# First head pair from all tokens, kept tokens chosen by 0/1 products, in masked attention on one core

## Chip, cores and metric

The kernel runs on one core of one Trainium2 chip. The core has TensorE (PE), with its weight loads shown on a row of their own (PEld), VectorE (DVE), ScalarE (ACT), GpSimd (POOL) and SyncE (SP), which here only issues DMAs. The metric is the device time of one execution in microseconds (us); the runs of the kernel before took 684.1, 685.0 and 688.35 us, median 685.0.

## The reference, cut to what matters

```python
B, D, T = x.shape                      # 8, 512, 1024, float32; NH = 8 heads of dk = 64
xt = jnp.transpose(x, (0, 2, 1))
q = xt @ Wq.T                          # one projection serves as queries, keys and values
qh = q.reshape(B, T, NH, dk).transpose(0, 2, 1, 3)
scores = scale * jnp.einsum('bhqd,bhkd->bhqk', qh, qh)
logits = (scores * cmask + (1.0 - cmask) * NEG) * rmask     # mask is 0 or 1
attn = jax.nn.softmax(logits, axis=-1)
ctx = jnp.einsum('bhqk,bhkd->bhqd', attn, qh)
out = ctx.transpose(0, 2, 1, 3).reshape(B, T, D) @ Wo.T
return x + jnp.transpose(out, (0, 2, 1))
```

About half of the 1024 tokens of a batch are kept (mask 1). All tokens that are not kept attend evenly to all tokens, so one column, the mean of x, stands for all of them.

## The kernel before

**Path.** `early` (L1014) counts the kept tokens of every batch. `late(n)` (L1137) computes with n columns a batch: up to n-1 kept tokens and the mean's column. n is 544 (`SHORT`) here, or 576 (`LONG`) in another branch; if neither fits, or if a sum of exponentials underflows, the general kernel is run at the end. Every engine reads `verdict` and branches between `early` and `late`. With n = 544 the columns lie in two halves of 272, and in four key chunks of 128 and one short chunk (`LAST`).

**Batches and pairs.** Heads are taken two at a time (128 rows). `pairs` holds 8 batches x 4 pairs; `p` counts them, `pr` is the pair in its batch `b`. A pair takes five steps k, one for each key chunk, the short one first. In a step `scores` puts q.q products into PSUM (tag `s`, two tiles of two banks; all other products share four banks of tag `t`), ACT takes exp of them, and then `slots_of(p)` and the tables after L1160 say what else is issued in the step: projecting and transposing a coming pair (`project`, `values`, `lengths_of`, `bias_of`), weighing the values of the pair before, output products, and the loading, transposing, gathering and fetching of other batches. This order is written out by hand; each engine runs its instructions in it. The second pair starts with the second row of L648, the short chunk's scores.

**The tokens of a batch.** Tokens are transposed to rows in DRAM (`xd`), the index of each kept token is found (`search`, DVE, by ranks), POOL gathers the rows by an indirect DMA (`gather`), PE transposes them back into `xc` (`collect`), and `project` multiplies by wqT. For batches 1 to 7 this runs beside the pairs of the batch before.

**The first batch.** Nothing runs beside it. `early` loads x of batch 0 on SP (L379, eight pieces of 256 KB), makes ranks (L1087), transposes all tokens (`turn_first`, L401: 32 transposes on PE, copies on ACT, stores on SP), sums features (`mean_first`, DVE) and searches. `late` loads wq on POOL, brings its columns into order (`order_columns`, ACT, L999), gathers, collects, transposes wq (`turn_weights`, L1009), projects pair 0 and half of pair 1, and only then begins the steps of pair 0.

**Number format.** All is float32. A plain product is recorded as two passes on PE, each with a weight load of its own; a transpose is recorded as one.

Of the kernel before, what the change touches and what calls it, by code (L numbers as in the profile page):

```python
# [19 lines left out]
NEG = -1e30  # L20
# [286 lines left out]
def attention_of_kept_tokens(ctx, tc, x, mask, wq, wo, out, ident, wqT, woT, verdict, flag):  # L307
# [52 lines left out]
    homes = [keep.tile([B * NT, P], F32, name=f"home_{i}") for i in range(2)]  # L360
    seen = {}
# [39 lines left out]
    def turn_first(i):  # L401

        r, at = divmod(i * P, NB)
        pt = bank(f"xt_0_{i}")
        for d in range(ND):
            nc.tensor.transpose(pt[:, d * P : (d + 1) * P], xs[0][r][:, d, at : at + P], ident)  # L406
# [58 lines left out]
    def place_ranks(b):  # L465
        rank = sb.tile([P, T], F32, tag="rank", name=f"rank_{b}", bufs=1)
        found = sb.tile([P, NC], F32, tag="found", name=f"found_{b}")
        if b:
            source = sb.tile([P, NC], I32, tag="source", name=f"source_{b}")
        else:  # L470
            source = keep.tile([P, NC], I32, name="source_0")
# [36 lines left out]
    def collect(b, i):  # L508
# [11 lines left out]
        )  # L520

# [79 lines left out]
    def bias_of(pair):  # L601
# [7 lines left out]
        biases[pair] = sb.tile([P, NC], F32, tag="bias", name=f"bias_{b}_{pr}")  # L609
# [325 lines left out]
    def slots_of(p):  # L935

        b, pr = pairs[p]
# [8 lines left out]
        if p == 0:  # L946
            todo[0].append(lambda: project(behind, 1))
            todo[1].append(lambda: values(behind))
        if behind:
            if p == 0:  # L950
                todo[2].append(lambda: lengths_of(behind))
            elif p != ND - 1:
                todo[1].insert(0, lambda: lengths_of(behind))
# [448 lines left out]
```

## Time and profile before

| | us |
|---|---|
| median of 3 runs | 685.0 |
| profiled execution | 689.0 |
| its span on the core | 687.3 |
| PE idle in the span | 41.7 |
| first scores of pair 0 (L648) | 40.06 |
| first scores of pair 1 | 58.11 |
| first scores of pair 2 | 72.97 |
| POOL's first gather | 22.90 |
| ACT's first instruction in `late` | 21.98 |

A page of the profile shows one execution. Busy times are unions over an engine's instructions. In the list by time, a row gives start, duration, engine, source line, operation, output and inputs, shapes and count, and in brackets the idle time before it with what ended it; rows of like instructions are merged, so the duration of a row with xN is that of all N. A matmul's recorded duration includes its way through the array, so the pace of a series is read from start to start. The clock column is TensorE's granted clock, 1.00 at full speed.

### The profile page before, as it was taken

Reading aid. Unit: us, or ns where it says so; the run is one execution under the profiler, and the core shown is the slowest. Engines: PE = TensorE matmul, PEld = TensorE weight load, DVE = VectorE, ACT = ScalarE, POOL = GpSimd, SP = SyncE. Lnnn points to the kernel's source line nnn. Section 1 sums busy time; section 2 is a strip of 40 time slices with the busy share of each in tenths; the row PEclk is TensorE's granted clock in tenths of the full one; section 3 lists DMA queues with packets and bytes.
Section 4 is the critical chain, followed back from the end, with each engine's and each line's share of the span. In section 5 each row is a group of like instructions: output and inputs, shape, how many; then the busy total and the mean of one; then the engine's idle time right before and its main releaser. Section 6 shows DMA issues by size and latency. Waiting matters only on the chain.

```text
span 687.3 us, 12044 instructions
## 1 busy us (share of the span) xinstructions
PE 645.6 (94%) x4139; PEld 391.5 (57%) x4139; DVE 359.4 (52%) x1049; ACT 397.2 (58%) x1059; POOL 182.5 (27%) x306
## 2 busy tenths in 40 slices
PE   6489999999999999999999999999999999999953
PEld 5456566656565655556565655555565656554422
DVE  5235676335464654747464654836564434724462
ACT  4566668755584657655584656665675556454400
POOL 3540310130044202450144202450144102334040
PEclk9799999999999999999999999999999999999985
DMA  6473832451766568854876477865764473339358
GB/s 230 155 240 90 253 89 68 141 158 45 169 182 212 155 171 209 269 181 115 210 191 207 156 182 193 261 193 137 190 195 127 114 184 100 113 119 251 84 174 260
DMA packets 96969, 116.37 MB, mean 169 GB/s; under 512 B 10312, under 2 KB 74312, under 8 KB 96896
## 3 DMA queue, kind: packets, MB, share of 16 engines
q1 hardware_dynamic: 80144, 75.13, 40.4%
q0 software_dynamic: 12528, 38.25, 17.4%
q10 hardware_dynamic: 4224, 2.10, 1.0%
q8 instruction: 35, 0.57, 0.3%
q14 instruction: 38, 0.31, 0.1%
HBM read 72.78 MB, written 42.67 MB: 168 GB/s over the span
## 4 chain that ended last, share of the span: by engine, by line
PE 84%; DMA 6%; ACT 3%; DVE 2%; issue 2%; SPq 1%; POOL 1%; POOLq 0%; ACTq 0%; DVEq 0%
PE s L626 21%; PE av L672 19%; PE pq L544 16%; PE po L793 14%; PE s L648 3%; PE xc L513 3%; PE v L569 2%; PE pa L821 2%; PE top L605 1%; ACT e L634 1%; DMA xr<-in_x_dram 1%; DMA xd<-xt 1%; DMA row<-rt 1%; DMA g<-od,origin 1%; PE xt L406 1%
## 5 line engine op out<-in xcount | busy, mean ns | idle before, releaser
L634 ACT ACTIVATE e<-s,bias 128x544 f32<-128x544 f32 x256 | 180.4, 710 | 69.4 <-PE s L626 63.2
L626 PE MATMUL s<-qT 64*128 64x272 f32 x1024 | 170.1, 417 | 2.9 <-ACT el L651 1.0
L626 PEld LDWEIGHTS s<-qT 64*128 64x128 f32 x1024 | 97.7, 186 | 70.6 <-issue 28.9
L672 PE MATMUL av<-e,v 128*64 128x272 f32 x1024 | 131.4, 399 | 0.0
L544 PE MATMUL pq<-xc,wqT 128*128 128x272 f32 x512 | 124.8, 397 | 0.0
L544 PEld LDWEIGHTS pq<-xc,wqT 128*128 128x128 f32 x512 | 97.4, 195 | 18.6 <-issue 0.8
L793 PE MATMUL po<-woT,cT 128*128 128x512 f32 (+1 forms) x448 | 107.5, 434 | 0.0
L672 PEld LDWEIGHTS av<-e,v 128*64 128x64 f32 x1024 | 67.9, 136 | 56.0 <-issue 23.1
L805 POOL DMA_DIRECT2D od<-oc x56 | 30.2, 551 | 251.3 <-ACT oc L803 251.1
L793 PEld LDWEIGHTS po<-woT,cT 128*128 128x128 f32 (+1 forms) x448 | 46.9, 150 | 46.9 <-issue 46.1
L907 POOL DMA_INDIRECT g<-od,block_origin x56 | 57.0, 1017 | 27.1 <-issue 12.4
L867 DVE STREAM_TRANSPOSE o<-g 128x512 f32<-128x512 f32 x56 | 39.3, 702 | 42.6 <-DMA g<-od,block_origin 42.6
L651 ACT ACTIVATE el<-s,bias 128x544 f32<-128x544 f32 x32 | 22.8, 714 | 59.8 <-PE s L648 44.9
L663 DVE CUSTOM_DVE_ANT_0 junk<-el,part 128x272 f32<-128x272 f32 x64 | 28.3, 442 | 53.4 <-ACT el L651 41.2
L592 DVE TENSOR_REDUCE len<-sq 128x10 f32<-128x640 f32 x32 | 26.2, 818 | 52.3 <-ACT sq L590 52.3
L552 ACT COPY qT<-pq 128x272 f32<-128x272 f32 x64 | 24.4, 381 | 49.9 <-PE pq L544 48.3
L903 POOL COPY step<-e 1x1 f32<-1x1 f32 x77 | 15.9, 206 | 136.2 <-ACT e L634 105.7
L634 ACT ACTIVATION_READ_ACCUMULATOR e<-s,bias 128x1 f32 x256 | 50.3, 197 | 0.0
L500 POOL DMA_INDIRECT xin<-xd,source x40 | 39.5, 987 | 20.3 <-issue 6.9
L870 DVE TENSOR_TENSOR xr<-o,xr 128x512 f32<-128x512 f32 x56 | 38.8, 693 | 9.9 <-DMA xr<-in_x_dram 6.9
L607 DVE TENSOR_REDUCE m<-top 128x1 f32<-128x128 f32 x32 | 9.3, 291 | 63.4 <-PE top L605 63.4
L488 DVE TENSOR_SCALAR_CACHE_REDUCE junk<-rank,key 128x1024 f32<-128x1024 f32 (+4 forms) x40 | 40.0, 999 | 3.4 <-ACT rank L1094 2.4
(147 smaller groups left out, 671.0 us busy)
## 6 DMA issues: line engine op xcount, KB each, us to landing
x<-in_x_dram SPq DMA_DIRECT2D x56, 256.0 KB
xd<-xt SPq DMA_DIRECT2D x112, 128.0 KB
xr<-in_x_dram SPq DMA_DIRECT2D x28, 512.0 KB
out_dram<-xr SPq DMA_DIRECT2D x24, 512.0 KB
rb<-row SPq DMA_DIRECT2D x60, 160.0 KB
od<-oc POOLq DMA_DIRECT2D x28, 256.0 KB
rank<-ranks SPq DMA_DIRECT2D x6, 512.0 KB
xd<-xt SPq DMA_DIRECT2D x8, 256.0 KB
```

What stands on the lines that cost most here:

```text
L488: nc.vector.tensor_scalar(junk[:, :n], rank[:, i * P :], key[:, col], 0.0, ALU.is_le, ALU.add, accum_out=found[:, col])
L500: nc.gpsimd.indirect_dma_start(out=xin[:n, :], out_offset=None, in_=xds[b], in_offset=bass.IndirectOffsetOnAxis(ap=searches[b][2][:n, i : ...
L544: nc.tensor.matmul(pq[:, :KH], wqT[:, d, pr * P : (pr + 1) * P], xcs[b][:, d, cols], start=(d == 0), stop=(d == ND - 1),)
L626: nc.tensor.matmul(ss[h][:, hf, :KH], qT[heads[h], keys], qT[heads[h], queries[hf]], start=True, stop=True,)
L634: nc.scalar.activation(e[:, :, h, :], ss[h][:, :, :KH], AF.Exp, bias=bias, scale=SCALE, accum_out=sums[pair[1] % 2][:, h, c : c + 1],)
L663: nc.vector.tensor_tensor_reduce(junk[:, :KH], e[:, 0, h, :], parts[b], 1.0, 0.0, ALU.mult, ALU.add, ends[pr % 2][:, h : h + 1])
L672: nc.tensor.matmul(av[head, :KH], v[keys, c, head], e[keys, hf if c < LAST else 0, h, :], start=(c == first), stop=(c == last),)
L793: nc.tensor.matmul(po[k * n : (k + 1) * n, :w], cTs[b, pr][:, i * P : i * P + n], woT[:, pr, k * w : (k + 1) * w], start=(pr == 0), stop=( ...
L805: nc.gpsimd.dma_start(ods[b][places[i], k * w : (k + 1) * w], oc[k * n : (k + 1) * n, :w])
L867: nc.vector.transpose(o.rearrange("p k t -> p (k t)"), gs[b, i])
L870: nc.vector.tensor_tensor(to, o, to, ALU.add)
L907: nc.gpsimd.indirect_dma_start(out=g, out_offset=None, in_=ods[b], in_offset=bass.IndirectOffsetOnAxis(ap=block_origin[:, b, i : i + 1], a ...
```

## The change

- x of batch 0 is loaded second half first, behind the first 128 rows of wq; the other rows of wq follow. They go into the room of `woT`.
- Pair 0 is projected from all 1024 tokens (`project_all`, eight blocks of 128 tokens) with those 128 rows of wq, transposed. DVE builds 0/1 matrices that say which token goes to which column (`choose`), and PE multiplies the projected blocks by them (`choose_of`) into `rings[0]`. The squares of all projected tokens give the pair's bias.
- The indices of the kept tokens come from products of the 0/1 matrices with a column of token numbers, and the mean of x from products of the transposed tokens with a column of ones (`tokens_of_first`). The ranks' broadcast, the search and the feature sums of batch 0 go.
- `late` begins with the steps of pair 0. Transposing wq, collecting the gathered tokens, projecting pairs 1 and 2 and the mean's column for pair 0 are issued within them. The projection of pair (1, 0) moves from the third pair to the fourth, and batch 1's loads, features, turns, gathers and collects move later by some steps.
- wq's columns are ordered on POOL; batch 1 is loaded on SP.
- The branch is taken on `fit < 544` alone; the 576 path is run behind it, inside the branch that holds the general kernel.

```diff
+    def load_first():
+
+        xs[0] = [sb.tile([P, ND, NB], F32, tag="x", name=f"x_0_{r}", bufs=NN) for r in range(NN)]
+        for r in reversed(range(NN)):
+            for d in range(ND):
+                nc.sync.dma_start(
+                    xs[0][r][:, d, :],
+                    x[0].rearrange("(p d) t -> d p t", d=ND)[d][..., r * NB : (r + 1) * NB],
+                )
+
+    def first_block(i):
         r, at = divmod(i * P, NB)
+        return [xs[0][r][:, d, at : at + P] for d in range(ND)]
...
-        for d in range(ND):
-            nc.tensor.transpose(pt[:, d * P : (d + 1) * P], xs[0][r][:, d, at : at + P], ident)
-        if i == 0:
-            xds[0] = dr.tile([T + 1, D], F32, tag="xd_0", name="xd_0", bufs=1)
-            nc.sync.dma_start(xds[0][T : T + 1, :], zero)
+        for d, block in enumerate(first_block(i)):
+            nc.tensor.transpose(pt[:, d * P : (d + 1) * P], block, ident)
         tag = "oc" if i < NC else "xin"
-        xt = sb.tile([P, D], F32, tag=tag, name=f"xt_0_{i}", bufs=NC)
-        nc.scalar.copy(
+        xt = firsts[i] = sb.tile([P, D], F32, tag=tag, name=f"xt_0_{i}", bufs=NC)
+        engine(
             xt.rearrange("p (a d f) -> p a d f", a=A, d=ND),
             pt.rearrange("p (d a f) -> p a d f", d=ND, a=A),
         )
         nc.sync.dma_start(xds[0][i * P : (i + 1) * P, :], xt)
 
-    def mean_first():
-        xbars[0] = keep.tile([P, ND, NN], F32, name="xbar_0")
-        for r in range(NN):
-            nc.vector.tensor_reduce(xbars[0][:, :, r], xs[0][r], axis=AX.X, op=ALU.add)
...
+    def choose(i, S):
+
+        nc.vector.tensor_scalar(S, count[:, : S.shape[1]], place[:, i : i + 1], None, ALU.is_equal)
...
+    def tokens_of_first(chosen, ones):
+
+        pt = bank("source_0")
+        for i in range(NC):
+            n = min(P, LONG - i * P)
+            for c in reversed(range(i, NT)):
+                nc.tensor.matmul(
+                    pt[:n, i : i + 1],
+                    chosen[c][:, i * P : i * P + n],
+                    since[:, c : c + 1],
+                    start=(c == NT - 1),
+                    stop=(c == i),
+                )
+        source = keep.tile([P, NC], I32, name="source_0")
+        nc.vector.tensor_scalar(source[:, :LAST], pt[:, :LAST], float(T), None, ALU.add)
+        nc.vector.tensor_scalar(source[:DK, LAST:NC], pt[:DK, LAST:NC], float(T), None, ALU.add)
+        searches[0] = None, None, source
+        pm = bank("mean_0")
+        for a in range(A):
+            for i in range(NT):
+                nc.tensor.matmul(
+                    pm[:, a : a + 1],
+                    firsts[i][:, a * P : (a + 1) * P],
+                    ones[:, 0:1],
+                    start=(i == 0),
+                    stop=(i == NT - 1),
+                )
+        nc.scalar.mul(first_mean, pm[:, :A], 1.0 / T)
...
+    def project_first(chosen, mcol):
+
+        wT = sb.tile([P, ND, P], F32, tag="junka", name="wqT_0", bufs=1)
+        pw = bank("wq_0_t")
+        for d in range(ND):
+            nc.tensor.transpose(pw[:, d * P : (d + 1) * P], woT[:, 0, d::ND], ident)
+        nc.scalar.copy(wT.rearrange("p d e -> p (d e)"), pw)
...
+        def project_all(i):
+            r, at = divmod(i * P, NB)
+            for d, block in enumerate(first_block(i)):
+                nc.tensor.matmul(
+                    tall[:, r, at : at + P], block, wT[:, d, :], start=(d == 0), stop=(d == ND - 1)
+                )
+
+        def copy_two(i):
+            r, at = divmod(i * P, NB)
+            nc.scalar.copy(
+                q[:, i : i + 2, :].rearrange("p c e -> p (c e)"), tall[:, r, at : at + 2 * P]
+            )
...
+        def choose_of(i):
+            w = chosen[i].shape[1]
+            for hf in range(2):
+                n = min(w - hf * H, H)
+                if n > 0:
+                    nc.tensor.matmul(
+                        short[:, hf, :n],
+                        q[:, i, :],
+                        chosen[i][:, hf * H : hf * H + n],
+                        start=(i == NT - 1),
+                        stop=(i * P <= hf * H),
+                    )
+
+        copy = nc.scalar.copy
+        for i in (7, 6, 5, 4):
+            project_all(i)
+            if i % 2 == 0:
+                copy_two(i)
+        turn_first(7, copy)
+        choose_of(7)
+        choose_of(6)
+        turn_first(6, copy)
+        square(1)
+        choose_of(5)
+        choose_of(4)
+        lengths(1)
+        turn_first(5, copy)
+        turn_first(4, copy)
+        for i in (3, 2, 1, 0):
+            project_all(i)
+            if i % 2 == 0:
+                copy_two(i)
+        for i in (3, 2, 1, 0):
+            choose_of(i)
+        square(0)
+        lengths(0)
+        nc.scalar.copy(
+            rings[0][:, :LONG].rearrange("p (h n) -> p h n", h=2), short[:, :, :H]
+        )
+        nc.vector.tensor_tensor(
+            first_len,
+            first_len,
+            mcol[:, :NT].unsqueeze(2).to_broadcast([P, NT, 2]),
+            ALU.mult,
+        )
+        nc.vector.tensor_reduce(
+            first_top, first_len.rearrange("p c h -> p (c h)"), axis=AX.X, op=ALU.max
+        )
+        turn_first(3, nc.vector.tensor_copy)
+        tops[pairs[0]] = first_top
+        bias_of(pairs[0], first_bias)
+        for i in (2, 1, 0):
+            turn_first(i, nc.vector.tensor_copy)
...
+    def put_first_mean():
+
+        xcs[0] = sb.tile([P, ND, NK], F32, tag="xc", name="xc_0", bufs=1)
+        nc.scalar.copy(xcs[0][:, :, NK - 1], first_mean)
+
+    def project_first_mean():
+
+        pq = bank("mean_0_0")
+        for d in range(ND):
+            nc.tensor.matmul(
+                pq[:, 0:1],
+                wqT[:, d, 0:P],
+                xcs[0][:, d, NK - 1 : NK],
+                start=(d == 0),
+                stop=(d == ND - 1),
+            )
+        nc.scalar.copy(rings[0][:, W - 1 : W], pq[:, 0:1])
...
         late = p == 2
         if pr == 2 and b + 1 < B:
-            at = (2, 2, 2, 3, 3) if late else (1, 2, 2, 2, 2)
+            at = (3, 3, 4, 4, 4) if late else (1, 2, 2, 2, 2)
             todo[at[0]].append(lambda: put_mean(b + 1))
             for i in range(NC):
                 todo[at[i]].append(lambda i=i: collect(b + 1, i))
+        if p == 0:
+            for d in range(ND):
+                todo[d // 2].append(lambda d=d: turn_weights(wqT, "wq", d))
+            todo[2].append(lambda: values(pair))
+            todo[2].append(put_first_mean)
+            for i in range(NC):
+                todo[(3, 3, 4, 4, 4)[i]].append(lambda i=i: collect(0, i))
+            for hf in range(2):
+                todo[4].append(lambda hf=hf: project(behind, hf))
+            todo[4].append(lambda: values(behind))
+            todo[4].append(lambda: lengths_of(behind))
+            for hf in range(2):
+                todo[4].append(lambda hf=hf: project(ahead, hf))
+            todo[4].append(project_first_mean)
+            todo[4].append(lambda: bias_of(behind))
+        elif p == 1:
+            todo[0].insert(0, lambda: values(behind))
+        elif p == ND - 1:
+            for hf in range(2):
+                todo[1 + hf].append(lambda hf=hf: project(behind, hf))
...
-        if ahead:
+        if ahead and p and not late:
             for hf in range(2):
-                todo[4 if late else 3].append(lambda hf=hf: project(ahead, hf))
-        if ahead and not late:
+                todo[3].append(lambda hf=hf: project(ahead, hf))
...
-            nc.scalar.copy(
+            nc.gpsimd.tensor_copy(
...
-        load_batch(0)
+        nc.sync.dma_start(woT[:, 0, :], wq[0:P, :])
+        load_first()
+        for e in range(1, ND):
+            nc.sync.dma_start(woT[:, e, :], wq[e * P : (e + 1) * P, :])
...
+        pc = bank("place_t")
+        nc.tensor.matmul(pc[:, :NT], upto, mcol[:, :NT], start=True, stop=False)
+        nc.tensor.matmul(
+            pc[:, :NT], spread[:, 0, :], before[:, 0, :], start=False, stop=True
+        )
...
+        room = room.rearrange("p k n -> p (k n)")
+        chosen, end = {}, 0
+        for i in reversed(range(NT)):
+            n = min((i + 1) * P, LONG)
+            chosen[i] = room[:, end : end + n]
+            end += n
+            choose(i, chosen[i])
...
+        project_first(chosen, mcol)
+        tokens_of_first(chosen, ones)
...
-        weights["wq"] = order_columns(load_weights(wq, "wq", nc.gpsimd), "wq")
+        queries_of(0)
+        load_batch(1)
+        weights["wq"] = order_columns([woT[:, e, :] for e in range(ND)], "wq")
+        for qT in rings[1:]:
+            nc.gpsimd.memset(qT[:, NK - 1 : NK], 0.0)
         for i in range(NC):
             gather(0, i)
-        queries_of(0)
-        for qT in rings:
-            nc.gpsimd.memset(qT[:, NK - 1 : NK], 0.0)
-        load_batch(1, nc.gpsimd)
         load_ranks(1, nc.gpsimd)
-        put_mean(0)
-        for i in range(NC):
-            collect(0, i)
-            if i < ND:
-                turn_weights(wqT, "wq", i)
         weights["wo"] = load_weights(wo, "wo", nc.gpsimd)
-        for hf in range(2):
-            project(pairs[0], hf)
-        values(pairs[0])
-        lengths_of(pairs[0])
-        project(pairs[1], 0)
+        qT = qTs[pairs[0]] = rings[0]
+        biases[pairs[0]] = first_bias
+        nc.vector.tensor_copy(
+            qT[:, NK:W].rearrange("p (r k) -> p r k", k=END),
+            qT[:, NK - END : NK].unsqueeze(1).to_broadcast([P, (W - NK) // END, END]),
+        )
...
+        LOAD_LATER = {(2, 1): (0, 1), (2, 2): (2, 3), (2, 3): (4, 5), (2, 4): (6, 7)}
+        TURN_LATER = [(0, 4), (1, 0), (1, 1), (1, 2)]
...
+        FEATURES_LATER = {(1, 1): (0,), (1, 2): (1,), (1, 3): (2,), (1, 4): (3,), (2, 0): (4, 5), (2, 1): (6, 7)}
...
+        GATHER_LATER = {(1, 4): (0,), (2, 0): (1,), (2, 1): (2,), (2, 2): (3,), (2, 3): (4,)}
...
-    with ExitStack() as pools:
-        early, late = attention_of_kept_tokens(
-            pools, tc, x, mask, wq, wo, out, ident, wqT, woT, verdict, flag
-        )
-        with tc.manual_schedule():
-            early()
-        fit = nc.values_load(verdict[0:1, 0:1], min_val=0, max_val=2 * T)
-        with tc.If(fit > SHORT - 1, label="over") as over:
-            with tc.If(fit < LONG):
+    def kept_tokens(n):
+
+        with ExitStack() as pools:
+            early, late = attention_of_kept_tokens(
+                pools, tc, x, mask, wq, wo, out, ident, wqT, woT, verdict, flag
+            )
+            with tc.manual_schedule():
+                early()
+            fit = nc.values_load(verdict[0:1, 0:1], min_val=0, max_val=2 * T)
+            with tc.If(fit < n):
                 with tc.manual_schedule():
-                    late(LONG)
-        with over.Else():
-            with tc.manual_schedule():
-                late(SHORT)
+                    late(n)
+
+    kept_tokens(SHORT)
     again = nc.values_load(flag[0:1, 0:1], min_val=0, max_val=1)
     with tc.If(again > 0, label="again"):
-        turn_all_weights(tc, [(wq, wqT), (wo, woT)], ident)
-        attention_of_all_tokens(tc, x, mask, out, ident, wqT, woT)
+        kept_tokens(LONG)
+        again = nc.values_load(flag[0:1, 0:1], min_val=0, max_val=1)
+        with tc.If(again > 0):
+            turn_all_weights(tc, [(wq, wqT), (wo, woT)], ident)
+            attention_of_all_tokens(tc, x, mask, out, ident, wqT, woT)
```

More of the change, by code (lines that the diff above doesn't have):

```diff
@@ L935, in slots_of @@
     def slots_of(p):
-        b, pr = pairs[p]
+        b, pr = pair = pairs[p]
         todo = [[] for _ in range(NC)]
@@ L1079, in early @@
         seen["mrow"], seen["rank"] = mrow, rank
-        tc.mark_branch_hint_location("over", "LikelyTaken", engines=ENGINES)
-        place_ranks(0)
-        for r in range(NN):
-            pt = bank(f"rank_{r}")
-            for i in range(G):
-                chunk = r * G + i
-                nc.tensor.matmul(
-                    pt[:, i * P : (i + 1) * P],
-                    ident[:BC, chunk : chunk + 1].to_broadcast([BC, P]),
-                    rank,
-                    start=True,
-                    stop=True,
-                )
-            nc.scalar.copy(searches[0][0][:, r * NB : (r + 1) * NB], pt)
-            if r == 0:
-                for i in range(NT):
-                    turn_first(i)
-        nc.vector.tensor_scalar(key[DK:P, LAST:NC], key[DK:P, LAST:NC], float(-DK), None, ALU.add)
+        nc.vector.tensor_tensor(place, pc[:, :NT], mcol[:, :NT], ALU.mult)
+        nc.vector.tensor_scalar(place, place, -1.0, None, ALU.add)
         nc.vector.tensor_copy(kept, pk[:, 0:B])
```

77 lines of the change are left out of this document (45 added, 32 removed).

## Prediction

> **What bounds the kernel now.** I read the page's busy table first, then busy time in stretches, the chain of waits, and PE's rows in order of time.
>
> ```profile
> PE 645.6 (94%) x4139; PEld 391.5 (57%) x4139; DVE 359.4 (52%) x1049; ACT 397.2 (58%) x1059; POOL 182.5 (27%) x306
> ```
> PE is busy for 94% of the span, so only its 41.7 us of idle time and its low-clock time can be won without removing PE work. The next view (stretch, length, then PE, PEld, DVE, ACT, POOL busy, PE's clock, DMA share, GB/s) says where the idle time is.
> ```profile
> 0.00:10.00 10.00, 6.33 (x26) 5.28 (x27) 5.66 (x26) 2.92 (x5) 3.98 (x18) 1.00 0.64 214
> 10.00:20.00 10.00, 5.32 (x33) 4.96 (x31) 6.97 (x12) 4.49 (x8) 2.20 (x4) 1.00 0.83 286
> 20.00:30.00 10.00, 3.82 (x25) 3.79 (x26) 2.00 (x9) 5.90 (x8) 5.78 (x6) 0.50 0.47 151
> 30.00:40.00 10.00, 8.94 (x51) 7.13 (x49) 0.98 (x2) 5.54 (x13) 7.57 (x17) 0.99 0.55 178
> ...
> 140.00:660.00 520.00, 516.11 (x3350) 302.92 (x3348) 275.33 (x793) 308.54 (x831) 142.00 (x234) 1.00 0.60 168
> ```
> 15.6 us of it lie in the first 40; from 140 to 660 only 3.9 are idle. So a shift of the start is carried to the end. The chain of waits (start, us, what) says what the start waits for:
> ```profile
> 14.98 7.01 DMA xd<-xt
> 22.90 3.43 DMA xin<-xd,source
> ...
> 32.31 3.88 PE pq L544 x16
> ```
> The transposed tokens are stored, gathered, and only then projected. PE's rows give the prices (start, us, line, shapes, count; a plain f32 product counts as two passes, a transpose as one):
> ```profile
> 5.25 0.59 PE L1074 MATMUL kept_t<-same,spread 64*128 64x8 f32 x2
> 5.70 0.56 PE L1075 MATMUL kept_t<-ones,spread 64*128 64x1 f32 x2
> 6.12 2.05 PE L1087 MATMUL rank<-rank_row,ident 64*128 64x128 f32 x8
> 8.10 6.13 PE L406 MATMUL xt<-ident,x 128*128 128x128 f32 x32
> ```
> From 5.70 to 6.12 one product with a single moving column takes 0.42 us: 0.213 a pass, as much as one with 128 columns. Its price is the load of 128 columns of weights. 24 of the transposes of L406 took 5.20 us in the chain, 0.217 each, before the clock rose; later 4 take 0.44, 0.11 each. So everything here halves at full clock: 0.11 for a pass of 128 columns, and for 272 columns 3.67/16 = 0.229 (L544 in the chain), 0.84 ns a column. Two rows mark the first pair's start and end:
> ```profile
> 40.06 0.69 PE L648 MATMUL s<-qT 64*64 64x272 f32 x8
> 58.11 0.69 PE L648 MATMUL s<-qT 64*64 64x272 f32 x8 [0.19 <-ACT e L634]
> ```
> The second pair starts at 58.1, and PE is dense after it. My sum asks when this comes after the change.
>
> **The change: PE's early work.** All four steps are on PE in program order ahead of the first scores.
> - Start. Four passes for `place_t` put the mask work's end at 6.26 + 4 x 0.213 = 7.1; four transposes of wq's first rows (0.85), the release (0.27) and ACT's copy (0.58, as L412) end at 8.9. The second half of x now comes first, behind one more piece of 256 KB: before, the first half was there at 8.2 and DVE read the second at 11.33, 0.8 a piece, so about 9.0 and 12.2. Start 9.0.
> - `project_all`: 32 products, 64 passes. Before, L406's pace doubled at 13.1, and the clock column changes at 19.9, 30.2, 50.6 and 54.1: all on steps of 3.41 us, and it rises after a step filled with PE work. Such a step may end here at 12.4 to 15.8; I take 14.1. Until then 24 passes at 0.213, the next 8 at 0.11: 15.0.
> - Sixteen transposes (1.8) and `choose_of` of blocks 7 to 4, 16 passes of 288 columns (0.242 each, 3.9): 20.7. Blocks 3 to 0: 32 passes (3.5) and 2560 pass-columns (2.15): 26.4. Sixteen transposes and the one of the bias (2.1): 28.5. The copies to SBUF (0.6 each on ACT or DVE) run beside it; bias and `rings[0]` are ready near 28.5.
> - `tokens_of_first`: 30 products for the indices (4 of them 64 wide) and 32 for the mean, one moving column each, so 120 full passes. Bounds for one: 0.07 (four transposes of 32 columns at L513 last 0.43, the last alone 0.22) and 0.213. I take 0.107, the 0.213 at twice the clock, since it is the same load: 12.8. First scores at 41.3, where they were at 40.1.
>
> [...]
>
> **The first pair.** Removed ahead of it: its projection (3.67), the first half of the second pair's, and the ranks' 16 passes (3.2). Put into it: 16 transposes of wq, the collects, all of the second and third pair's projections (3.67 each) and 8 passes for the mean's column. Its first part hangs on ACT: copy of the mean and reading the verdict 1.1, `el` and share 0.8, four chunks of exp at 1.4 (rows 0.70 apart), four copies of wqT at 0.5, v 0.75, three collects' copies 1.5, waits for scores 0.4: 12.2 (PE has 9.5 of work there). Then PE alone: 3.67, 0.4 for a copy, values 0.55, 3.67, the mean 0.86, the bias 0.3: 9.5. Sum 21.7, where it was 18.05 with a low-clock stretch of 3.4 us in it. The third pair's values (0.55) go to the second. 41.3 + 21.7 + 0.55 - 58.1 = **+5.4 us**.
>
> **What I cost at nothing.** `order_columns` goes from ACT (4.07) to POOL: 272 columns cost POOL 0.98 (L393), so at most 1.85 for each of four from 14.6 on (three more pieces after x), done by 22; the gathers behind it wait for the indices (35) anyway. Gathers 2 to 4 reuse buffers that the mean reads: issued from 41.3, 1.27 each, 3.4 to land (22.90 to 26.33): 48.5, and PE collects them near 51; should that cover go, each us late costs one. Batch 1's eight loads go from POOL to SP, behind the last stores (30.5), 0.45 each; landed by 40, first read past 50. `choose` on DVE (3584 columns, under 4.5 us by L488's 1.28 for 1024) runs from 8 to 13, its first block needed at 15.4. DVE's conversion of the indices waits for PE (34.5); behind it stand only memsets, `lacks` and the filling of `rings[0]`, done by 37. The zero row's store goes to POOL, ahead of nothing that is near. Pair (1, 0)'s projection moves from the third to the fourth pair, the same work in dense PE time; batch 1's collects move one slot later and its last gather to one slot ahead of its collect (about 3 us for 3.4 to land): 0 to 1, taken as 0. Batch 1's features (ACT) and a turn (DVE) move one pair later, where DVE is busy 8.4 to 9.2 of 10: 0 to 1 us, taken as 0. The late stage is now fallen into rather than jumped to. Before, ACT's compare at 16.0 was followed by its next instruction at 21.9, SP's 15.4 by 21.6, PE's 14.0 by 14.5. I take PE's; 6 us on ACT would cost about 5.
>
> The profiled execution lasts 689.0 (span 687.3 and 1.7 around it), 4.0 over the median 685.0. With +5.4 it would be 694.4, and the median 690.4.
>
> **Rivals.**
> - *The loads cost less.* At 0.07 a pass the phase takes 8.4, the scores start at 36.9, +1.0: 686. For it, the 32-column row; against it, that those are one-pass loads.
> - *The phase drops the clock.* After a stretch with 2.10 us of PE work out of 3.4 the clock was halved for 3.4 us:
> ```profile
> 43.81:47.23 3.42, 2.66 (x15) 1.50 (x13) 1.66 (x3) 3.30 (x10) 0.00 (x0) 1.00 0.57 177
> 47.23:50.64 3.41, 2.10 (x10) 1.19 (x11) 0.98 (x2) 3.41 (x12) 0.00 (x0) 1.00 0.50 110
> 50.64:54.05 3.41, 3.41 (x9) 2.58 (x9) 1.93 (x5) 1.40 (x5) 0.00 (x0) 0.50 0.14 28
> ```
>  One column per load may count as idle. Falling 3.9 us into the phase, 36 passes are done and 84 cost 0.213: scores at 50.3, and the first pair, cold at first, some 4 longer: +18.5, 703.5. For it, that hardly anything moves through the array; against it, that no row here shows what weight loads count for. [...]
> - *The other side: faster.* `mean` at L527 issued 8 passes in 0.29, less 0.19 for one: 0.013 each. At that price the phase takes 1.6, the scores start at 30.1, -5.7: 679. It decides from a first score before 35.8. Against it: those weights have 32 columns and different column groups. A clock that rises at 12.4 would add under 1 us.
> - *ACT's 6 us of code return*: 695.5.
> - *It does not do what it says*, that is, ends in the 576 path: the same counts took the 544 path before (272 columns a half). Over 730.
>
> **Numbers.** Forecast 0.40, cheap loads 0.15, low clock 0.25, faster 0.11, ACT's code 0.08, 576 path 0.01. The time is 690.5. The range, 681 to 706, leaves out most of the faster case and the low clock's upper part. About 1% is what a measurement can tell: 678.2 to 691.9. Faster 0.06 (the faster case with an early clock); slower 0.47 (low clock, ACT's code, a third of the forecast); same 0.47.
>
> **What would show it.** 124 passes for indices and mean between about 28 and 41, 0.107 apart (0.07, or 0.213 with the clock at 0.50, for the rivals); the first L648-type row near 41; the second pair's near 63.5; ACT without a gap past 1.2 us at the branch; then PE dense and the same tail. A first score before 35.8 makes the sign wrong; one after 46, the size.

## The result, and the profile after

| | before | after |
|---|---|---|
| median of 4 runs (us) | 684.96 | 715.34 |
| lowest to highest (us) | 684.1 to 688.35 | 711.71 to 716.65 |
| profiled execution (us) | 689.0 | 714.41 |
| its span (us) | 687.3 | 712.6 |
| PE idle in the span (us) | 41.7 | 36.5 |

The kernel became slower: ratio 1.0425, 95% interval 1.0372 to 1.0479. The profiled executions differ by 25.3 us of span, less than the medians do, because the profiled run of before lay 4.0 us above its median and that of after 0.9 below its own. The text below accounts for those 25.3.

PE's share of busy time rose (this is the page's busy table):

```profile
PE 676.1 (95%) x4331; PEld 421.0 (59%) x4331; DVE 358.8 (50%) x1049; ACT 392.8 (55%) x1055; POOL 181.9 (26%) x299
```

PE works 30.5 us more, and has 192 more instructions. Busy time in stretches (columns as in the prediction) shows what this busy time is made of:

```profile
20.00:30.00 10.00, 9.54 (x79) 9.05 (x76) 3.19 (x9) 2.96 (x6) 0.00 (x0) 1.00 0.23 84
30.00:40.00 10.00, 10.00 (x65) 9.97 (x64) 1.53 (x9) 0.00 (x0) 1.82 (x2) 0.65 0.88 296
40.00:50.00 10.00, 10.00 (x49) 10.00 (x48) 0.00 (x0) 0.00 (x0) 0.25 (x1) 0.50 0.14 48
140.00:660.00 520.00, 515.96 (x3386) 308.14 (x3383) 273.07 (x804) 318.83 (x865) 143.36 (x236) 1.00 0.64 172
```

From 40 to 50 the matmul row and the weight-load row are both busy 10.00 of 10, and still the granted clock is 0.50. The stretch from 140 to 660 is as dense as it was. PE's rows in order of time (start, us, line, shapes, count) name the work of the slow stretch:

```profile
29.00 8.39 PE L446 MATMUL source<-since,chosen 128*128 128x1 f32 x60
37.32 13.81 PE L460 MATMUL mean<-ones,xt 128*128 128x1 f32 x64
51.06 1.18 PE L801 MATMUL s<-qT 64*64 64x272 f32 x8
```

These are the products with one moving column for the indices and for the mean. They end at 51.06 with the first scores, and those themselves take 1.18 us where they took 0.69 before. Narrow stretches give the moment of the change:

```profile
29.00:32.93 3.93, 3.93 (x38) 3.93 (x37) 1.90 (x4) 0.00 (x0) 0.00 (x0) 1.00 0.77 277
32.93:36.34 3.41, 3.41 (x18) 3.41 (x17) 0.00 (x0) 0.00 (x0) 0.00 (x0) 0.51 0.93 291
43.20:51.10 7.90, 7.90 (x42) 7.88 (x41) 0.00 (x0) 0.00 (x0) 0.07 (x1) 0.50 0.00 0
```

In the first 3.93 us 38 passes were issued at 0.103 each, then 18 in 3.41, 0.19 each. The 64 of the mean took 13.74 to the first scores, 0.215 each from start to start; the record of one lasts 0.352. The clock was halved 3.9 us into the phase and came back near 56.8.

The first scores of the pairs (L648 before, L801 after) show where the 25.3 us arose:

| first scores of pair | 0 | 1 | 2 | 3 | 4 | 31 | end of span |
|---|---|---|---|---|---|---|---|
| before | 40.1 | 58.1 | 73.0 | 91.8 | 108.6 | 627.5 | 687.3 |
| after | 51.1 | 75.2 | 90.4 | 111.4 | 133.5 | 650.5 | 712.6 |
| difference | 11.0 | 17.1 | 17.4 | 19.6 | 24.9 | 23.0 | 25.3 |

There are three places: up to pair 1 (17.1), pairs 1 to 3 (7.8, of which 7.5 in pairs 2 and 3), and the tail (2.3). Between pairs 4 and 31 1.9 come back; all versions below run the same code there and took 516.9 (the changed kernel) to 529.4 us for it, so these 1.9 are within the scatter between runs. For the second place the chain of waits has one large piece:

```profile
102.99 1.04 PE xc L648 x8
104.03 0.27 issue
104.29 6.64 DMA xin<-xd,source
110.93 0.14 issue
111.07 0.40 PE xc L648 x4
111.47 1.06 PE s L801 x8
```

Batch 1's last gather takes 6.64 us to land, and PE's row at 111.07 waits 4.00 us for it. Before, batch 0's first gather landed in 3.43, with no load of x beside it. SyncE's queue shows what ran at that time:

```profile
101.58 4.38 SPq L385 DMA_DIRECT2D x<-in_x_dram  x8
```

Eight loads of x, 256 KB each, are issued from 2.7 us ahead of the gather on. The clock was halved again from 94.4 to 97.8, behind a wait of PE for ACT's copy `v` (1.34 us at 92.92), and from 111.4 to 114.9, behind the wait for the gather. On ACT a feature sum of batch 1 stands ahead of `el` and `v`:

```profile
90.98 0.62 ACT L589 ACTIVATE junka<-x 128x512 f32<-128x512 f32 x1
```

It puts `el` off by 0.6 us (from 90.98 to 91.59). In the kernel before, `el` of this pair follows the exp directly, and PE doesn't wait there.

### The profile page after: what moved, and what is told of

Its sections match the earlier page's. It is cut to its first block, busy times and chain, and to the rows that moved or that the text cites. A ratio compares the mean times of both kernels' runs of the same rounds, so it can differ in the third digit from the quotient of the medians.

```text
span 712.6 us, 12424 instructions
## 1 busy us (share of the span) xinstructions
PE 676.1 (95%) x4331; PEld 421.0 (59%) x4331; DVE 358.8 (50%) x1049; ACT 392.8 (55%) x1055; POOL 181.9 (26%) x299
## 4 chain that ended last, share of the span: by engine, by line
PE 78%; DMA 10%; DVE 4%; SPq 2%; ACT 2%; issue 1%; POOL 0%; ACTq 0%; DVEq 0%; POOLq 0%
PE s L779 18%; PE av L825 16%; PE po L946 13%; PE pq L697 13%; DMA xd<-xt 3%; PE xc L648 2%; PE s L801 2%; PE v L722 2%; PE mean L460 2%; PE pa L974 2%; DMA row<-rt 1%; PE tall L485 1%; DMA out_dram<-xr 1%; SPq L578 1%; PE source L446 1%
## 5 line engine op out<-in xcount | busy, mean ns | idle before, releaser
L787 ACT ACTIVATE e<-s,bias 128x544 f32<-128x544 f32 x248 | 175.0, 710 | 68.8 <-PE s L779 67.1
L779 PE MATMUL s<-qT 64*128 64x272 f32 x1024 | 168.0, 419 | 0.9 <-ACT e L787 0.7
L825 PE MATMUL av<-e,v 128*64 128x272 f32 x1024 | 132.9, 402 | 0.0
L697 PE MATMUL pq<-xc,wqT 128*128 128x272 f32 x496 | 119.3, 393 | 0.5 <-ACT xc L652 0.5
L697 PEld LDWEIGHTS pq<-xc,wqT 128*128 128x128 f32 x496 | 93.1, 193 | 18.3 <-issue 0.8
L745 DVE TENSOR_REDUCE len<-sq 128x10 f32<-128x640 f32 x31 | 25.3, 818 | 56.6 <-ACT sq L743 56.6
L705 ACT COPY qT<-pq 128x272 f32<-128x272 f32 (+1 forms) x62 | 23.7, 382 | 49.4 <-PE pq L697 49.4
L787 ACT ACTIVATION_READ_ACCUMULATOR e<-s,bias 128x1 f32 x248 | 48.6, 196 | 0.0
L570 DVE STREAM_TRANSPOSE xt<-x 128x1024 f32<-128x1024 f32 x28 | 34.7, 1240 | 3.8 <-DMA xd<-xt 3.7
```

Source lines behind the costliest of these rows:

```text
L570: nc.vector.transpose(xt.rearrange("p k (d f) -> p k d f", d=ND), xs[b][r][:, :, at : at + n].rearrange("p d (k t) -> p k d t", t=Q),)
L697: nc.tensor.matmul(pq[:, :KH], wqT[:, d, pr * P : (pr + 1) * P], xcs[b][:, d, cols], start=(d == 0), stop=(d == ND - 1),)
L779: nc.tensor.matmul(ss[h][:, hf, :KH], qT[heads[h], keys], qT[heads[h], queries[hf]], start=True, stop=True,)
L787: nc.scalar.activation(e[:, :, h, :], ss[h][:, :, :KH], AF.Exp, bias=bias, scale=SCALE, accum_out=sums[pair[1] % 2][:, h, c : c + 1],)
L825: nc.tensor.matmul(av[head, :KH], v[keys, c, head], e[keys, hf if c < LAST else 0, h, :], start=(c == first), stop=(c == last),)
```

## The experiments

**Theory.** The products with one moving column let the clock fall, the loads of x beside the last gather cost most of pairs 2 and 3, and the jump over the second branch lengthens the tail. **Rivals.** The phase is slow for another reason, such as the price of the loads themselves; the 7.5 us come from the features that were moved; the tail's difference is chance. Most versions have one run. In pairs 4 to 31 single runs differ by up to 12 us, with PE's waits for `top` of DVE (in the stretch from 140 to 640, 1.0 us in all in the changed kernel and up to 7.2 in others); up to pair 1 four runs of the same code differ by 0.9 (74.3 to 75.2). So the first scores of the early pairs are the measure, and the total only supports it. Each experiment changes the changed kernel, unless another is named.

### More moving columns in the same products (100 and 128)

```diff
-                    pt[:n, i : i + 1],
+                    pt[:n, i * 100 : (i + 1) * 100],
-                    since[:, c : c + 1],
+                    since[:, c : c + 1].to_broadcast([P, 100]),
...
-                    pm[:, a : a + 1],
+                    pm[:, a * 128 : (a + 1) * 128],
-                    ones[:, 0:1],
+                    ones[:, 0:128],
```

> The products for the indices move 100 copies of their column and those for the mean 128 columns of ones, so each of the 124 passes has the same weights and about a hundred times the moving work; the results used are the same. Theory (the clock counts what moves through the array, not the loading of weights, so one moving column lets it fall): the clock stays at 1.00, the 124 passes take 13 to 14 us (0.107 to 0.115 each) instead of 22.1, the first scores come at 42 to 43 instead of 51.1, the second pair near 65 instead of 75.2, time about 704. Rival (the clock falls for another reason, or a pass costs 0.21 whatever moves): the mean's passes stay at 0.213, first scores at 51 or later, time 714 or more.

It took 707.5 us (before, on the same chip, 692.41 in one run). PE's rows:

```profile
29.15 6.79 PE L446 MATMUL source<-since,chosen 128*128 128x100 f32 x60
35.87 7.41 PE L461 MATMUL mean<-ones,xt 128*128 128x128 f32 x64
43.22 0.69 PE L804 MATMUL s<-qT 64*64 64x272 f32 x8
```

With about a hundred times as many columns to stream, the same 124 passes took 14.1 us instead of 22.1, 0.112 and 0.115 each, and the clock was 1.00 throughout. Pair 1 began at 65.4 (75.2 in the changed kernel), pair 8 at 199.9 (209.5). That fits the theory: a pass with one column, 0.103 at full clock, cost nearly what one with 100 or 128 did, so in these runs it paid for its load; and with one column the clock was 0.50 while the weight-load row was busy 7.88 us of 7.90.

### 32 and 64 moving columns

The same edit with 32 in both places, and then with 64.

> The same with 32 moving columns in both: the array streams for about a quarter of a pass. If a quarter is too little for the clock (it was halved in the kernel before after a stretch with about 0.95 us of streaming in 3.4), the clock falls as in the changed kernel: first scores near 51, time about 714. If anything above nearly nothing suffices: as with 128 columns, first scores near 42, time about 704.

> As the kernel with 32 moving columns in the single-column products, with 64 in both. The array then streams for half of each pass. With 32 the clock fell, with 100 and 128 it stayed. If half is enough: first scores at 43, time near 705. If not: first scores at 51, time near 714.

PE's rows and stretch with 32 columns:

```profile
36.91 13.86 PE L461 MATMUL mean<-ones,xt 128*128 128x32 f32 x64
```
```profile
40.00:50.00 10.00, 10.00 (x49) 10.00 (x48) 0.00 (x0) 0.00 (x0) 0.00 (x0) 0.50 0.14 40
```

With 64 columns:

```profile
36.16 7.36 PE L461 MATMUL mean<-ones,xt 128*128 128x64 f32 x64
```
```profile
40.00:50.00 10.00, 10.00 (x78) 7.78 (x78) 3.34 (x10) 5.63 (x15) 5.54 (x9) 1.00 0.51 146
```

With 32, the phase is that of the changed kernel: first scores at 50.7. The total, 720.51, is 6 above what was expected; pairs 4 to 31 took 522.0 us in this run. With 64 it is that of 128: first scores at 43.5, pair 1 at 65.1, total 702.4. So in this series the border lies between 32 moving columns (clock 0.50 from 40 to 50) and 64 (1.00); at an equal number of instructions and loads only the moving columns differ. The quarter and the half of a pass in the two expectations are estimates: at the prediction's 0.84 ns a column, 32 columns make 27 ns of a pass of 104, and 64 make 54 of 114. The 0.95 us of streaming was the author's estimate too; no row shows it, only 2.10 us of PE work in that stretch of 3.41.

### The mean by VectorE's sums

The 64 mean passes are replaced by two sums on DVE and 8 small passes, as the kernel before did it.

```diff
+        mean_of(0)
         pm = bank("mean_0")
-        for a in range(A):
-            for i in range(NT):
-                nc.tensor.matmul(pm[:, a : a + 1], firsts[i][:, a * P : (a + 1) * P], ones[:, 0:1], ...)
+        for d in range(ND):
+            nc.tensor.matmul(pm[d * Q : (d + 1) * Q, :A], within, xmeans[0][:, d, :], ...)
...
+        mean_first(1)
         lengths(1)
+        mean_first(0)
```

> The mean of x is made as in the kernel before: two reductions on DVE (2.3 us each, in DVE's idle time between 16.9 and 26) and 8 passes with 32 columns of weights; the 64 single-column passes go. Theory (those passes stand on the path at 0.213): first scores 13 us earlier, near 38, at the half clock that the index products have caused; second pair near 62, time about 701. Rival (the gathers, not PE's products, hold the first pair): the gathers' landing keeps the second pair at 70 or later, time 709 or more.

The first scores came at 39.0 and pair 1 at 63.0, both 12 earlier than in the changed kernel, so the gathers do not hold the first pair here. The index passes alone still lowered the clock: from 33.30 to 36.70 it was 0.65 and then 0.50. But the time, 713.57, is not lower by 12. The lead stood at pair 9 (212.5 against 224.4), was down to 4 at pair 30 (630.3 against 634.4) and gone at pair 31 (650.8 against 650.5): from 340 to 640 PE was busy 294.56 us of 300 where the changed kernel had 298.23, with the clock falling near 533 and again near 642. In that stretch PE waits twice for `top` of DVE, 3.8 us in all (1.0 in the changed kernel); behind the longer wait, 2.31 us at 531.84, `pq` takes 5.52 us at half clock instead of 3.83. Ahead of pair 31 PE waits 1.84 us for ACT. Why these waits are longer in this run was not tested; with one run of each, it can't be told from the scatter between runs. The total was a miss.

### The loads of x behind the last gather

```diff
-LOAD_LATER = {(2, 1): (0, 1), (2, 2): (2, 3), (2, 3): (4, 5), (2, 4): (6, 7)}
+LOAD_LATER = {(2, 4): (0, 1, 2, 3), (3, 1): (4, 5), (3, 2): (6, 7)}
```

> Batch 2's loads of x are issued from the last step of the third pair on instead of from its second, so they no longer run beside batch 1's last gather. Collision theory (the gather lands 6.6 us after its issue because 2 MB of x are loading): it lands in about 3.4 us, PE's wait of 4.0 us in the third pair falls under 1, the clock dip behind it goes, time 709 to 711. Rival (the gather is simply issued one step ahead of its use): the wait stays near 4, time 714.

In the chain of waits the last gather now reads

```profile
103.81 3.77 DMA xin<-xd,source
107.71 0.40 PE xc L648 x4
108.12 0.62 PE s L801 x8
```

It lands 2.87 us sooner, PE waits 0.55 and 1.11 instead of 0.53 and 4.00, and the scores behind it run at full clock (0.62 for what took 1.06). While it landed, 0.68 MB of other transfers were moved beside it, where it had been 1.88. Pair 4 began at 129.0 instead of 133.5, pair 8 at 205.2 instead of 209.5; total 712.34. This run was 0.5 ahead at pair 2 already; counted from there, pair 4 comes 4.1 sooner and pair 8 3.8. That is what the collision is worth of the 7.5.

### The features back to their old place

```diff
-FEATURES_LATER = {(1, 1): (0,), (1, 2): (1,), (1, 3): (2,), (1, 4): (3,), (2, 0): (4, 5), (2, 1): (6, 7)}
+FEATURES_LATER = {(1, 0): (0,), (1, 1): (1,), (1, 2): (2, 3), (1, 3): (4,), (1, 4): (5,), (2, 0): (6,), (2, 1): (7,)}
```

> Batch 1's feature sums (ACT) are spread from the first step of the second pair on, one or two a step, so that two are left for the third pair instead of four. Theory (four sums beside two exps a step fill ACT in the third pair, PE waits 1.34 us there and loses the clock for 3.4 us): that wait and the dip go, third pair 2 to 3 us shorter, time 2 to 3 us less, 712. Rival (the second pair's ACT has no room either): the second pair grows by what the third gains, 714.

Nothing came of it: pair 4 at 133.8, total 714.21, PE's wait for the last gather 4.15. But one feature sum stands ahead of `el` in this run too (at 90.12 on ACT), and PE's wait of 1.34 for `v` and the low clock behind it stay. So spreading the other sums is worth nothing, and what the one that stayed costs was not tested. That the features cost all of the 7.5 us can't be, by the run before this one.

### Gathers, loads and features together

```diff
-GATHER_LATER = {(1, 4): (0,), (2, 0): (1,), (2, 1): (2,), (2, 2): (3,), (2, 3): (4,)}
+GATHER_LATER = {(1, 4): (0, 1, 2), (2, 0): (3,), (2, 1): (4,)}
```

and both edits above.

> Three placings at once: batch 1's gathers as early as in the kernel before, batch 2's loads after them, features spread. Theory: what the changed kernel loses between the start of the second and of the fifth pair (75.2 to 133.5, 58.3, where the kernel before has 58.1 to 108.6, 50.5) is these waits and dips and nothing else, so the 58.3 falls to 50 to 52; the single-column phase stays, first scores at 51; time 707. Rival (the moved projection of the fifth pair's tokens or DVE's turns cost it): it stays above 55.

PE no longer waits for any of batch 1's gathers, and pair 4 begins at 127.3, total 711.51. From pair 1 to pair 4 it now takes 52.7 us (74.6 to 127.3), the changed kernel 58.3, the kernel before 50.5. So placing explains 5.6 of the 7.8 us that were lost between pairs 1 and 4, a little less than was expected (50 to 52, total 707). PE's wait of 1.34 for `v` and the low clock behind it are still there.

### Both cures

The products with 100 and 128 columns, and the three placings.

> The wide products (100 and 128 moving columns, same results) and the three placings together. If the two causes add: first scores at 43, second pair at 65.4, fifth pair at 115 to 117, about 8 behind the kernel before, time 695 to 699. Rival (they share a cause): no better than the better of the two, 704 or more.

The granted clock of the page (40 slices of the span) is now whole up to the tail:

```profile
PEclk9999999999999999999999999999999999999985
```

The changed kernel's begins `9959`. First scores 43.1, pair 1 at 64.8, pair 4 at 117.3, pair 31 at 634.9; total 699.8, the best single run of a version with these products. Before, on the same chip, had a median of 684.74 in 7 runs. The profiled spans, 698.1 and 687.3, differ by 10.8: 6.7 at pair 1, 2.0 more at pair 4, 1.3 of it back by pair 31, and 3.4 in the tail. Neither the clock nor the collision is in it. Two waits of PE lie between pairs 1 and 4:

```profile
82.52 0.68 PE L828 MATMUL av<-el,v 64*64 64x272 f32 x4 [1.34 <-ACT v L733]
...
91.88 0.32 PE L761 MATMUL top<-ident,top 128*128 128x128 f32 x1 [1.37 <-DVE top L755]
```

Their sum is 2.71; before has waits of 1.30 between the same pairs (1.09 the longest). So waits make about 1.4 of the 2.0 lost there. Ahead of the `v` of the first one a feature sum stands on ACT again (at 80.58). No run took these waits away.

### No products with one column

Keeps the placing of the run above. The indices come again from ranks and DVE's search, the mean from DVE's sums, as in the kernel before; the first pair is still projected from all tokens.

```diff
-        tokens_of_first(chosen, ones)
+        mean_first(0)
+        mean_of(0)
...
+        spread_ranks()
         choose_of(7)
...
+        for i in range(NC):
+            search(0, i)
         lengths(1)
+        mean_first(1)
```

> The three placings, and no single-column products at all: the indices come from the search on DVE with ranks spread by 16 passes, the mean from DVE's sums and 8 passes inside the first pair, as in the kernel before; the projection of all of x and the choosing by 0/1 products stay. Theory: the first scores come when the projection, choosing and transposes end plus 1.8 for the ranks, near 31; second pair near 53.5 (58.1 before), fifth pair near 105 (108.6); time 3 to 5 us under the kernel before. Rival (the gathers, started after the last store at 31, become what the first pair waits for): second pair at 58 or later, no gain.

It took 705.52 us (698.4 to 706.6), ratio to before 1.027, interval 1.0193 to 1.0348: slower, where a gain was expected. PE's row:

```profile
36.67 1.18 PE L799 MATMUL s<-qT 64*64 64x272 f32 x8 [5.37 <-DVE qT L1318]
```

PE was done with its early work at 31.3, and then waited 5.37 us for DVE, where the filling of `rings[0]` stood behind the second feature sum; the clock was halved from about 36.3 to 43.1. A second version moves the sums up in DVE's queue and puts three copies of turned tokens on ACT:

```diff
-        mean_first(0)
         mean_of(0)
...
+        mean_first(1)
         for i in range(NC):
             search(0, i)
         lengths(1)
-        mean_first(1)
+        mean_first(0)
...
-            turn_first(i, nc.vector.tensor_copy)
+            turn_first(i, copy)
```

> The version without single-column products, with DVE's order mended: both feature sums go into DVE's idle time (from 17 and from 25.6), and the last three transposed blocks are copied by ACT, so that DVE reaches the filling of rings[0] at about 33 instead of 36.4 and PE has no gap in which its clock falls. Theory: first scores at 32.5 to 33.5, clock at 1.00 throughout, second pair 21.7 later at 54.5 to 55.5 (58.1 in the kernel before), fifth pair at 107 to 109 (108.6); with a tail 2.4 longer the time is within 3 of the kernel before. Rival (the gathers, issued after the last store has landed near 36, hold the first pair): second pair at 58 or later, time 4 or more over it.

It took 699.54 us (697.1 to 706.58), ratio 1.0222, interval 1.0136 to 1.0308, again slower. PE's rows:

```profile
32.87 0.69 PE L800 MATMUL s<-qT 64*64 64x272 f32 x8 [1.51 <-DVE qT L1318]
...
42.89 0.66 PE L647 MATMUL xc<-ident,xin 128*128 128x128 f32 x4 [2.06 <-DMA xin<-xd,source]
44.38 1.08 PE L647 MATMUL xc<-ident,xin 128*128 128x128 f32 x4 [0.84 <-DMA xin<-xd,source]
45.40 2.19 PE L778 MATMUL s<-qT 64*128 64x272 f32 x8
...
61.40 0.69 PE L800 MATMUL s<-qT 64*64 64x272 f32 x8
```

The first scores come 7.2 us earlier than in the kernel before, and yet pair 1 starts 3.3 later. The first pair must collect the gathered tokens, and the first gather was issued at 36.12, where it was issued at 22.90 before: SP's stores of the turned tokens now reach from 16.24 to 32.47 (9.87 to 15.34 before), since the turning stands among the projection. PE waits for the gathers within the pair, the clock falls (0.53 from 43 to 54), and the gain is gone.

The late issue is not all of it. Behind the stores SP issues batch 1's loads of x:

```profile
32.76 3.89 SPq L385 DMA_DIRECT2D x<-in_x_dram  x8
```

The DMA share from 33 to 43 is 1.00, and the first gather lands 6.72 us after its issue, at 42.84, where PE's first wait ends. Landed in 3.43 as before, it would have been there at 39.6, ahead of 40.8, when PE was ready for it (an estimate). So the collision that batch 1's last gather meets in the changed kernel is probably here too; a run with these loads behind the gathers was not made.

### The branch as it was

Both cures, with the branch structure and the branch hints of the kernel before: the usual path stands in the `Else`, and one test follows it.

```diff
-            with tc.If(fit < n):
+        with tc.If(fit > SHORT - 1, label="over") as over:
+            with tc.If(fit < LONG):
...
+        with over.Else():
+            with tc.manual_schedule():
+                late(SHORT)
```

> The wide products and three placings, with the branches of the kernel before: a jump over the 576 path into the 544 path at the start, and one jump over the general kernel at the end. Theory (a jump over much code costs an engine 3 to 6 us until its next instruction, and the second jump at the end is what makes the tail 2.3 us longer): the tail from the last pair's start shrinks from 63.2 to about 61, but ACT comes 3 to 6 us later to the first exp, second pair at 68 to 71 instead of 64.8; time 700 to 704 (699.8 without). Rival (the hints hide the jumps): second pair at 65, time 697.

ACT's row behind the branch:

```profile
47.71 0.71 ACT L807 ACTIVATE el<-s,first_bias 128x544 f32<-128x544 f32 x1 [3.46 <-issue]
```

Its operand had been there since 44.6. The idle time ends by nothing that the profile shows; it lies right behind the branch. From the compare to the next instruction the engines took 5.1 (POOL), 3.2 (SP), 3.6 (DVE), 0.5 (PE) and 2.9 us (ACT); in the changed kernel ACT's compare was followed by its next instruction after 0.06. So the gaps go with the jump; what the engines do in them was not shown.

The time was 709.89, more than was expected. Pair 1 began at 70.7, 5.9 later than with both cures, PE waiting 2.14 for ACT and the clock falling after it. The first scores, ahead of ACT's branch, were already 0.9 later (43.97 against 43.12), so falling through is worth about 5.1 us at the start. Another 6.6 were lost in pairs 4 to 31, within the scatter there.

From pair 31 to the end of the span it took 60.6 us, against 63.2 with both cures, 62.1 in the changed kernel and 59.8 before. The eleven runs that end with two tests took 61.0 to 63.2 for this tail. So a longer tail goes with the second test, by 2.1 us on the mean of the two kinds. From SP's last DMA issue to the end, where the tests stand, it is 1.1 (mean 7.5 with two tests; 6.1 and 6.8 with one). How much of it is the second jump itself was not shown.

## Why the prediction was wrong

It forecast 690.5 and up to 706; the time was 715.34.

**The step that failed: the price of a pass in `tokens_of_first`.** The sum put 120 passes at 0.107, 12.8 us, with the clock at full speed. There were 124 passes in 22.06 us (29.00 to 51.06), the greater part at 0.215. The second rival had the mechanism and nearly its size: the clock falling 3.9 us into the phase (measured 3.93), first scores at 50.3 (51.06), +18.5 at pair 1 (+17.1). It was given 0.25. The reason against it was that no row showed what weight loads count for; that was an unknown, and its two answers lay 13 us apart at pair 1, so the sum rested on a guess. Its price at full clock was right: 0.103 in the first 38 passes, 0.112 to 0.115 with 100 and 128 columns. It was half of 0.213, taken as a price at half clock, though the clock column shows 1.00 there. The pace bears that out: the transposes that take 0.217 each at 8.10 take 0.215 where the column shows 0.50 (26.46 to 29.90 in the kernel before), and 0.11 at 1.00. The rival's 703.5 would still have been too low by what comes behind pair 1, 8.2 us (7.8 - 1.9 + 2.3), and by the 4.0 and 0.9 by which the profiled runs lie off their medians.

**With the clock kept, the sum holds.** In the run with both cures the first scores are at 43.1 (41.3 forecast), and the first pair takes 64.8 - 43.1 = 21.7, the figure of the sum; its two parts, split where PE begins to project the second pair (55.28), take 12.2 and 9.5, as in the sum. Together +6.7 at pair 1 and +7.1 at pair 2, where +5.4 was forecast with the values that move to the second pair. `project_all` started at 8.84 (9.0), the source phase at 29.00 (28.5). So of the 17.1 us at pair 1, 10.4 were the low clock: 8.0 before the first scores, and 2.4 in the first pair (24.1 against 21.7). The wide passes are themselves a little dearer than the first 38, by about 1.3 us over the phase (an estimate: 14.1 less 124 x 0.103), so the low clock may have cost up to 11.7.

**"Taken as 0" was wrong for batch 1's gathers.** The range of 0 to 1 us looked at the gather's time alone (about 3 us for 3.4 to land). It didn't ask what else the DMA engines carry then: 2 MB of x, which run beside it. That cost 3.8 to 4.1, and all placings together 5.6. Of the features the same was said; one of their sums puts PE's `v` off by 0.6 us (an estimate from ACT's rows), and in the changed kernel the clock fell behind that wait. No run moved this sum, so its cost stays open.

**The tail was called the same.** It is 2.3 longer, and the runs put that down to the end with its second test, though not to the us. The prediction costed the branch at its start only, where it was right: no engine lost time there (ACT's gap 0.06 us), and the rival of 6 us on ACT fell. It did not follow the branch to its end.

**Right.** The gathers that wait for the mean (POOL idles 10.78 us until then) and `order_columns` on POOL (4.29 us, done at 16.2) set no later end; the 544 path was taken.

**The account** of the 25.3 us: the low clock to pair 1 10.4, the early work that stays at full clock 6.7, pairs 1 to 3 7.8 (of which placing 5.6), back in the steady part -1.9 (scatter), tail 2.3; together 25.3. Of the remaining 2.2 us in pairs 1 to 3 the two waits for ACT and DVE shown above make about 1.4, net of what before waits there; that they are the cause was not shown.

**Why no version won.** At full clock, `tokens_of_first` alone holds PE 14.1 us in a time when it idled before. Taken out, the first scores come early, but the first pair then waits for gathers that are issued 13.2 us later than before and land in 6.7 us instead of 3.4.

## What to carry to other kernels

Here a pass with one moving column cost nearly what one with 128 did (0.103 and 0.115 us at full clock), and in a series of 124 the clock fell to 0.50 and the price rose to 0.215. So price such a series by its passes and at both clocks; give it as many columns as kept the clock (here 64, with loads of 128), or do the sum on another engine. When a transfer is moved, ask what else is on the DMA engines in its new place, and not only whether its own time fits. When work is brought ahead of a wait, look at what the moved work pushes back: here projecting first delayed the stores, and with them the gathers that the first pair needs to end, until they ran beside the loads of the next batch.

## What the runs showed of the hardware

- From 43.20 to 51.10 in the changed kernel PE's matmul and weight-load rows were busy 7.90 and 7.88 us of 7.90, and the granted clock was 0.50. In these series of 124 float32 passes 1 and 32 moving columns for each load let the clock fall to 0.50, 64, 100 and 128 kept it at 1.00. So the busy time of the profile's rows did not decide it.
- A pass with 128 columns of weights took 0.103 us with one moving column at full clock and 0.215 with 1 or 32 at half; with 64 to 128 it took 0.108 to 0.115 at full clock (8 of these 124 passes load 64 columns). The loads of 128 columns are recorded with 192 ns (median, L446 from 29.0 to 32.9) at full clock and 333 (L460) at half.
- In the run with the branches of the kernel before, the branch over the 576 path took ACT, SP, DVE and POOL 2.9 to 5.1 us to the next instruction and PE 0.5; in the changed kernel, which falls through, ACT's came after 0.06.
- Batch 1's last indirect gather landed in 3.77 us beside 0.68 MB of other transfers and in 6.64 beside 1.88 MB; the first gather of the kernel before, with no load beside it, in 3.43.
